# Group-norm moments of x in the prologue: half of the groups moved from VectorE to ScalarE and TensorE

## The chip, the cores and the metric

The kernel runs on one core of one Trainium2 chip. The metric is the device time of one execution in microseconds (us); the time given for a kernel is the median of its runs.

## The reference

Two attention layers, each behind a group norm with a residual add, on x of shape (1, 128, 256, 256) in fp32. Cut to what matters:

```python
def _gn(v, G=32, eps=1e-5):                    # 32 groups of 8 channels
    g = v.reshape(B_, H_, W_, G, C_ // G)
    m = jnp.mean(g, axis=(1, 2, 4), keepdims=True)   # over all rows and the 8 channels
    s = jnp.var(g, axis=(1, 2, 4), keepdims=True)
    return ((g - m) / jnp.sqrt(s + eps)).reshape(v.shape)

x = x + _L0_conv_ref(_gn(x), z, ...)   # row attention, 8 heads; bias b = layer_norm(z) @ Wb.T
x = x + _L1_conv_ref(_gn(x), ...)      # banded attention, 4 heads, |i - j| <= 16
return x
```

Layer 0 needs the mean and variance of every group of x over the whole tensor before its first row can be normalised. It also needs the bias b, made from z of shape (1, 256, 256, 128), before its first softmax.

## The kernel before

The kernel has a prologue, then layer 0, then layer 1. Layers 0 and 1 walk over 64 pairs of rows. The change lies in the prologue alone, except for its effect on when layer 0 can start.

**The loop of the prologue.** It runs over 16 z jobs (`zjobs`, n = 0 to 15) of 2 MB each. In the turn of job n:

- `z_front(n)` loads the z tile `zt` (three buffers, SyncE's queue, L1090), takes its row moments on VectorE (`bn_stats`, L1107), and has GpSimd raise the variances to the power -1/2 (`zrs`, L1115);
- `z_back(n-1)` transposes the z tile of the job before on TensorE (L1128, 32 transposes into the three PSUM tiles `ps_t`), copies the transposes to SBUF on ScalarE (`zT`, L1130, 8 copies), and multiplies them by the small weight (`z_project`, L1143). The projection runs half a job behind. Every second job also makes a copy `bT` (L1152), a scaling `bt` on VectorE (L1161) and eight exponentials into `eb` on ScalarE (`z_exp`, L1172);
- `x_block(n-1)`, in the turns n = 1 to 8, loads 4 MB of x into `xa` (two buffers, SyncE's queue, L1179) and takes the moments of its 32 groups on VectorE: 16 `bn_stats`, each of two groups (L1181).

`weights()` prepares the weights in steps between these. `load(4)` issues four small weight loads on ScalarE's queue (L832) in each of the turns 1 to 5, before that turn's `z_back`.

**After the eighth block of x** (n = 8, held in `ended`), a hand-written `plan` attaches steps to places (turns after `ended`, quarter of that turn's `z_front`; quarter 4 is the end of the turn). `begin` runs `x_moments`, which merges the blocks' moments on VectorE; `moments_steps` then averages over partitions on TensorE (`gps_l`, L972 and L981), and `norm` makes M0 and R0. `weigh` takes the moments of layer 0's first pair and calls `root` on GpSimd (`lrs`, L1288) and `send`, one quarter later in the plan, sends the result to DRAM from ScalarE's queue (L1294).

From n = 8 on, `z_back(n)` is also done in its own turn. Before the change this happens after `x_block`:

```python
            if nx < n and nx < nga:
                x_block(nx)
                ...
            if ended is not None:
                z_back(*behind)
                behind = None
            mark(4)
```

The prologue runs in a written order: each engine executes its instructions in the order of this text. An engine that waits holds up everything that follows on it. The prologue ends where layer 0 makes its first scores (`ps_sc`, L1367).

The functions that the diff touches, and what calls them:

Of the kernel before, what the change touches and what calls it, by code (L numbers as in the profile page):

```python
# [9 lines left out]
F32 = mybir.dt.float32  # L10
AF = mybir.ActivationFunctionType
ALU = mybir.AluOpType
AX = mybir.AxisListType
# [3 lines left out]
P = 128  # L17
# [4 lines left out]
def bcast(ap, axis, n):  # L22

    ap = ap.unsqueeze(axis)
    shape = list(ap.shape)
    shape[axis] = n
    return ap.broadcast_to(shape)
# [746 lines left out]
def fast_kernel(  # L774
# [25 lines left out]
    nc = tc.nc  # L800
    S, I, C = x.shape
# [4 lines left out]
    G = 32  # L806
    GE = C // G
    NB = I // P
# [12 lines left out]
    ones = const.tile([P, P], F32, name="ones")  # L821
    nc.vector.memset(ones, 1.0)
    avg = const.tile([P, P], F32, name="avg")
# [6 lines left out]
    def load(n):  # L830
        for _ in range(min(n, len(queued))):
            nc.scalar.dma_start(*queued.pop(0))  # L832
# [80 lines left out]
    GA = min(16, S)  # L913
# [17 lines left out]
    for a in range(KC):  # L931
        for h in range(H1):
            n = P // H1
# [5 lines left out]
    for h in range(H1):  # L939
        n = P // H1  # L940
# [22 lines left out]
    def group_pairs(src, g):  # L963

        return src[:, :, g * GE : (g + 2) * GE].rearrange("p n (h e) -> p n e h", h=2)

    def moments_steps(run, n, pool, psum, tag):

        ps = psum.tile([P, 512], F32, name=f"gps_{tag}", tag="mm")
        mean_p = pool.tile([P, G], F32, name=f"mean_{tag}", tag="gn_a", bufs=1)  # L970
        nc.vector.tensor_copy(mean_p, run[:, :, 1])
        nc.tensor.matmul(ps[:, :G], avg, mean_p, start=True, stop=True)  # L972
        yield
        mu = pool.tile([P, G], F32, name=f"mu_{tag}", tag="gn_b", bufs=1)
        nc.vector.tensor_copy(mu, ps[:, :G])
        d = pool.tile([P, G], F32, name=f"d_{tag}", tag="gn_c", bufs=1)
        nc.vector.tensor_sub(d, mean_p, mu)
        nc.vector.tensor_mul(d, d, d)
        nc.vector.scalar_tensor_tensor(d, run[:, :, 2], 1.0 / n, d, ALU.mult, ALU.add)
        ps2 = psum.tile([P, 512], F32, name=f"gps2_{tag}", tag="mm")  # L980
        nc.tensor.matmul(ps2[:, :G], avg, d, start=True, stop=True)  # L981
        yield
        rs = pool.tile([P, G], F32, name=f"rs_{tag}", tag="gn_d", bufs=1)
        nc.vector.tensor_scalar_add(rs, ps2[:, :G], 1e-5)
        nc.gpsimd.tensor_tensor(rs, rs, mhalf[:, :G], ALU.pow)
        yield
        M = const.tile([P, C], F32, name=f"M_{tag}")
        R = const.tile([P, C], F32, name=f"R_{tag}")
        for dst, src in ((M, mu), (R, rs)):
            nc.vector.tensor_copy(dst.rearrange("p (g e) -> p g e", e=GE), bcast(src, 2, GE))  # L990
        yield M, R

    pz = tc.alloc_tile_pool(name="pre_z", bufs=1, side="right")
    px = tc.alloc_tile_pool(name="pre_x", bufs=1, side="left")
    ps_mm = tc.alloc_tile_pool(name="ps_mm", bufs=2, space=PSUM)
    pps = tc.alloc_tile_pool(name="pre_ps", bufs=2, space=PSUM)

    def mm(name):
        return ps_mm.tile([P, 512], F32, name=name, tag="mm")
# [71 lines left out]
        nc.vector.tensor_add(bout_r, bout_r, ps[:, :C])  # L1071

    nga = S // GA
    st0 = pz.tile([P, nga, G, 3], F32, name="st0")

# [40 lines left out]
    def z_back(b, i0, zt, rs):  # L1118

        nonlocal turned  # L1120
        at = i0 % IS
        for j in range(at // 16, (at + IB) // 16):
            zTs = []
            for g in range(4):
                ps_t = pps.tile([P, 512], F32, name="ps_t", tag="zT", bufs=3)
                i = (4 * j + g) * 4 - at
                for a in range(4):
                    nc.tensor.transpose(ps_t[:, a * P : (a + 1) * P], zt[:, i + a, :], ident)  # L1128
                zT = pz.tile([P, 512], F32, name="zT", tag="zT", bufs=10)
                nc.scalar.copy(zT, ps_t)  # L1130
                zTs.append(zT)
            z_project()
            turned = (b, i0 - at, rs, j, zTs)

    def z_project():
        nonlocal turned, ps_b
        if turned is None:
            return
        (b, i0, rs, j, zTs), turned = turned, None
        if j == 0:  # L1140
            ps_b = pps.tile([P, 512], F32, name="ps_b", tag="bias", bufs=1)
        for g in range(4):
            nc.tensor.matmul(  # L1143
                ps_b[32 * g : 32 * (g + 1), :], wbz[:, j].rearrange("p a h -> p (a h)"), zTs[g],
                start=(j == 0), stop=(j == 3),
            )
        if j == 1:
            z_exp()
        if j < 3:
            return  # L1150
        bT = pz.tile([P, 512], F32, name="bT", tag="bT", bufs=2)
        nc.scalar.copy(bT, ps_b)  # L1152
        ps_k = pps.tile([P, 4, 4, 4, H], F32, name="ps_k", tag="keys", bufs=1)
        for a in range(4):
            nc.tensor.transpose(
                ps_k[:, a].rearrange("p g j h -> p (g j h)"), bT[:, a * P : (a + 1) * P], ident
            )
        bt = pz.tile([P, IS, H], F32, name="bt", tag="bt", bufs=2)
        for j in range(4):
            q = slice(j * 16, (j + 1) * 16)  # L1160
            nc.vector.tensor_tensor(  # L1161
                bt[:, q, :].rearrange("p (g a) h -> p g a h", g=4), ps_k[:, :, :, j, :].rearrange("p a g h -> p g a h"),
                bcast(rs[:, q].rearrange("p (g a) -> p g a", g=4), 3, H), ALU.mult,
            )
        weighed.append((b, i0, bt))
# [11 lines left out]
    def x_block(j):  # L1177
        xa = px.tile([P, GA * NB, C], F32, name="xa", tag="xa", bufs=2)
        nc.sync.dma_start(xa, x[j * GA : (j + 1) * GA].rearrange("s i c -> (s i) c").rearrange("(p n) c -> p n c", p=P))  # L1179
        for g in range(0, G, 2):  # L1180
            nc.vector.bn_stats(st0[:, j, g : g + 2, :].rearrange("p g f -> p (g f)"), group_pairs(xa, g))  # L1181

    def x_moments():

        each = GA * NB * GE
        run = pz.tile([P, G, 3], F32, name="run0")
        d = pz.tile([P, nga, G], F32, name="run0_d")
        nc.vector.tensor_reduce(run[:, :, 1], st0[:, :, :, 1].rearrange("p j g -> p g j"), AX.X, ALU.add)
        nc.vector.tensor_scalar_mul(run[:, :, 1], run[:, :, 1], 1.0 / nga)
        nc.vector.tensor_tensor(d, st0[:, :, :, 1], bcast(run[:, :, 1], 1, nga), ALU.subtract)  # L1190
        nc.vector.scalar_tensor_tensor(d, d, float(each), d, ALU.mult, ALU.mult)
        nc.vector.tensor_tensor(d, d, st0[:, :, :, 2], ALU.add)
        nc.vector.tensor_reduce(run[:, :, 2], d.rearrange("p j g -> p g j"), AX.X, ALU.add)
        return moments_steps(run, nga * each, pz, ps_mm, "l0")

# [355 lines left out]
    def weigh():  # L1553
# [5 lines left out]

    plan = {  # L1560
        (0, 4): begin, (1, 1): lambda: next(steps), (1, 3): lambda: next(steps), (1, 4): take, (2, 3): norm,
        (3, 4): weigh,
        (4, 2): lambda: now.send(nc.scalar),
        (4, 4): lambda: now.turn([mm("ps_x") for _ in range(KC)]),
        (5, 2): lambda: now.fetch(nc.scalar),
# [4 lines left out]
    ended = None  # L1570

    def mark(quarter):
        if n == 1 and quarter < 4 or n == 6:
            next(prepare, None)
        if ended is not None:
            plan.pop((n - ended, quarter), nothing)()


    behind, nx, n = None, 0, 0
    prepare = weights()  # L1580
    with tc.manual_schedule():
        zts = [z_load(*zjobs[0], 2)]
        load(8)
        zts.append(z_load(*zjobs[1]))
        for n, job in enumerate(zjobs):
            front = z_front(*job, zts.pop(0) if zts else z_load(*job))
            if n == 0:
                next(prepare)
                next(prepare)
            else:  # L1590
                load(4)
                if n == 1:
                    next(prepare)
            if behind is not None:
                z_back(*behind)
            behind = (*job, *front)
            if nx < n and nx < nga:
                x_block(nx)
                nx += 1
                if nx == nga:  # L1600
                    ended = n
            if ended is not None:
                z_back(*behind)
                behind = None
            mark(4)
        assert not plan
        z_project()
        z_exp()
        for f in ("centre", "scale"):
            getattr(nxt, f)()  # L1610
        for r in range(2):
            nxt.moments(r)
# [115 lines left out]
    with tc.tile_pool(name="l1", bufs=2) as sb, tc.tile_pool(  # L1728
        name="l1s", bufs=4
    ) as sm, tc.tile_pool(name="ps1_s", bufs=4, space=PSUM) as ps_s, tc.tile_pool(  # L1730
        name="ps1_o", bufs=1, space=PSUM
    ) as ps_o:

        def mm1(name):
            return ps_s.tile([P, 512], F32, name=name, tag="s")
# [348 lines left out]
        ps = mm1("ok_ps")  # L2084
# [67 lines left out]
```

## Time and profile before

| what | value |
|---|---|
| time before, median of 3 runs | 3188.46 us (3186.13 to 3190.39) |
| the profiled execution, its own time | 3190.91 us |
| its span in the trace | 3189.1 us |
| TensorE, VectorE, GpSimd, ScalarE busy over the span | 95%, 73%, 71%, 49% |
| first `ps_sc` matmul (end of the prologue) | 237.83 us from the span's start |
| VectorE on x's moments (`st<-xa`) | 128 instructions, 77.2 us |
| VectorE on z's moments (`zst<-zt`) | 256 instructions, 87.4 us |
| ScalarE's copies `zT` | 128 instructions, 66.9 us |

A row of the groups view reads: line, engine, operation, names, output shape, input shape, count, then busy us and mean ns of one, then the engine's idle time just ahead of these and what ended it. A row of the timeline reads: start in us, length in us, engine, line, operation, names, shapes, count, and in brackets the idle time before it with what ended that. Rows of the timeline merge several instructions.

### The profile page before, as it was taken

What the parts mean: (1) busy time and instruction counts of PE and PEld (TensorE: products, weight loads), DVE (VectorE), ACT (ScalarE), POOL (GpSimd) and SP (SyncE); (2) the same over time, 40 slices, a digit from 0 to 9 for tenths busy, and PEclk for the clock granted to TensorE, in tenths of its full rate; (3) what the DMA queues carried; (4) which work ended last, traced back from release to release, by engine and by line L of the source; (5) the groups of instructions that cost most, each with busy time, mean ns of one, the idle gap of its engine ahead of it and who ended that gap; (6) DMA issues with size and microseconds to landing.
All of it is one profiled execution on the core that took longest, in us unless ns stands there. A gap on an engine that the chain in (4) does not pass through costs nothing. (4 is left out here: it accounts for less than half of the span.)

```text
span 3189.1 us, 82775 instructions
## 1 busy us (share of the span) xinstructions
PE 3041.5 (95%) x34924; PEld 2086.6 (65%) x34924; DVE 2332.1 (73%) x3783; ACT 1551.1 (49%) x2501; POOL 2277.3 (71%) x1634
## 2 busy tenths in 40 slices
PE   4479999999999999999999999799999999999998
PEld 3245555555555555555555555588888888888886
DVE  7965677777777777777777777577777766666677
ACT  2354444444444444444444444355555555555553
POOL 3378888888988898888898987455555555555553
PEclk9789999999999999999999999899999999999999
DMA  9942333333333332333333432543434344434341
GB/s 349 393 159 53 70 91 96 97 71 95 96 97 71 98 93 66 93 91 97 71 97 94 97 71 61 108 101 82 102 82 96 87 95 88 96 88 93 90 96 47
DMA packets 691068, 328.56 MB, mean 103 GB/s; under 512 B 538656, under 2 KB 639904, under 8 KB 689536
## 3 DMA queue, kind: packets, MB, share of 16 engines
q1 hardware_dynamic: 686112, 320.28, 39.4%
q8 instruction: 276, 4.52, 0.6%
q10 hardware_dynamic: 4576, 2.90, 0.3%
q14 instruction: 104, 0.85, 0.1%
HBM read 254.36 MB, written 68.75 MB: 101 GB/s over the span
## 5 line engine op out<-in xcount | busy, mean ns | idle before, releaser
L1391 POOL TENSOR_TENSOR eboth<-e 128x512 f32<-128x512 f32 x512 | 743.4, 1472 | 186.6 <-PE ps_su L1410 100.4
L1387 DVE TENSOR_TENSOR e<-ps_sc,eb 128x1024 f32<-128x1024 f32 x384 | 458.3, 1221 | 297.4 <-ACT ps_sc L1379 297.4
L1908 POOL TENSOR_TENSOR e<-e,bw 128x384 f32<-128x384 f32 x256 | 258.0, 1028 | 501.1 <-ACT e L1906 501.1
L1379 ACT ACTIVATE ps_sc<-ps_sc 128x1024 f32<-128x1024 f32 x384 | 375.4, 1007 | 438.1 <-PE ps_sc L1367 314.0
L1367 PE MATMUL ps_sc<-qT,kT 32*128 32x256 f32 x4096 | 293.4, 400 | 1.8 <-ACT kT L1337 1.8
L1457 PEld LDWEIGHTS ps_y<-wo,oT 128*128 128x128 f32 x1024 | 195.3, 191 | 88.1 <-issue 44.4
L1333 PE MATMUL ps_p<-xnT,wq 128*128 128x512 f32 x512 | 249.4, 610 | 3.5 <-POOL xnT L1320 3.4
L1367 PEld LDWEIGHTS ps_sc<-qT,kT 32*128 32x128 f32 x4096 | 185.1, 184 | 103.2 <-issue 91.9
L1457 PE MATMUL ps_y<-wo,oT 128*128 128x256 f32 x1024 | 243.9, 381 | 7.1 <-POOL oT L1447 6.3
L1966 PE MATMUL ps_su_y<-w_out,oT 128*128 128x256 f32 x1024 | 244.7, 382 | 4.7 <-DVE odd L1944 2.8
L1333 PE MATMUL ps_p<-xgT,wg 128*128 128x512 f32 x512 | 248.9, 609 | 0.0
L1402 PE MATMUL ps_ov<-e,v 128*32 128x256 f32 x4096 | 248.7, 383 | 0.0
L1852 ACT ACTIVATE u<-ps_qk,bin_c 128x256 f32<-128x256 f32 x378 | 177.8, 478 | 132.3 <-PE ps_qk L1847 124.3
L1348 PE MATMUL ps_v<-wv,xnT 128*128 128x256 f32 x1024 | 241.9, 379 | 0.0
L1333 PE MATMUL ps_p<-xnT,wk 128*128 128x512 f32 x512 | 241.5, 594 | 0.0
L1883 PE MATMUL ps_v<-w_in,xgT 128*128 128x256 f32 x1024 | 238.3, 386 | 0.0
L1348 PEld LDWEIGHTS ps_v<-wv,xnT 128*128 128x128 f32 x1024 | 194.7, 190 | 55.1 <-issue 32.1
L1945 DVE RECIPROCAL rv<-odd 128x256 f32<-128x256 f32 x128 | 224.4, 1753 | 4.4
L1966 PEld LDWEIGHTS ps_su_y<-w_out,oT 128*128 128x128 f32 x1024 | 195.7, 191 | 32.9 <-DVE odd L1944 3.5
L1883 PEld LDWEIGHTS ps_v<-w_in,xgT 128*128 128x128 f32 x1024 | 189.3, 190 | 32.8 <-issue 0.5
L1402 PEld LDWEIGHTS ps_ov<-e,v 128*32 128x32 f32 x4096 | 120.4, 110 | 109.5 <-issue 43.9
L1847 PE MATMUL ps_qk<-dT,wst 128*128 128x256 f32 x756 | 187.7, 388 | 0.0
(201 smaller groups left out, 6027.7 us busy)
## 6 DMA issues: line engine op xcount, KB each, us to landing
xa<-in_x_dram SPq DMA_DIRECT2D x8, 4096.0 KB
xt<-in_x_dram SPq DMA_DIRECT2D x64, 512.0 KB
x<-xo SPq DMA_DIRECT2D x16, 2048.0 KB
xs<-x SPq DMA_DIRECT2D x256, 128.0 KB
xt<-x SPq DMA_DIRECT2D x64, 512.0 KB
rvb<-rsum SPq DMA_DIRECT2D x252, 128.0 KB
out_dram<-yo SPq DMA_DIRECT2D x63, 512.0 KB
xs<-in_x_dram SPq DMA_DIRECT2D x248, 128.0 KB
```

Source lines behind the costliest of these rows:

```text
L1333: nc.tensor.matmul(ps, w[:, k, m * P : (m + 1) * P], getattr(self, src)[:, k, :], start=(k == 0), stop=(k == KC - 1),)
L1348: nc.tensor.matmul(self.ps_v[:, b * C : (b + 1) * C], self.xnT[:, k, t * P : (t + 1) * P], wv[:, k, :], start=(k == 0), stop=(k == KC - 1),)
L1367: nc.tensor.matmul(self.pss[q // 2][:, q % 2, b, :], self.kT[rs, c, r * I + b * P : r * I + (b + 1) * P], self.qT[rs, c, r * I : (r + 1) * I],
L1379: nc.scalar.activation(self.pss[a], ps, AF.Exp)
L1387: nc.vector.tensor_tensor(es[a], pss[a], eb[:, h : h + 2], ALU.mult)
L1391: nc.gpsimd.tensor_tensor(t, es[a][:, :, 0, :], es[a][:, :, 1, :], ALU.add)
L1402: nc.tensor.matmul(ov[q * D0 : (q + 1) * D0, c, :], self.v[:, r, b, h * D0 : (h + 1) * D0], es[q // 2][:, q % 2, b, :], start=(b == 0), st ...
L1457: nc.tensor.matmul(self.ps_y[:, b * C : (b + 1) * C], self.oT[r][:, k, b * P : (b + 1) * P], wo[:, k, :], start=(k == 0), stop=(k == KC - 1),)
L1883: nc.tensor.matmul(ps[:, b * C : (b + 1) * C], self.xgT[:, k, t * P : (t + 1) * P], w_in[:, k, 2 * C : 3 * C], start=(k == 0), stop=(k == ...
L1908: nc.gpsimd.tensor_tensor(e[:, q], e[:, q], bcast(bw.rearrange("p b w -> p (b w)"), 1, KC), ALU.mult)
L1945: nc.vector.reciprocal(self.rv[:, r, :], odd[:, 2, :])
L1966: nc.tensor.matmul(ps[:, b], self.oT[r][:, k, b * P : (b + 1) * P], w_out[:, k, :], start=(k == 0), stop=(k == KC - 1),)
```

## The change

1. `x_block` gives VectorE only the first 16 groups: 8 `bn_stats` in place of 16.
2. For the other 16 groups ScalarE runs one `Square` activation per group over 256 elements of each partition, with a bias column `nm0` (minus a first guess of the mean) and an accumulated output `sq0`. The squares themselves go to a tile `junk` of one buffer. TensorE sums the same channels over all partitions with a matrix of ones (8 matmuls of 512 columns in four groups of 32 output partitions, accumulated in `ps_sx` over all blocks).
3. In the first block, `nm0` is made: one matmul by `avg` over four rows, one reduction and one scaling on VectorE.
4. `x_moments` and `moments_steps` merge both kinds. A second moment about the guess becomes a variance by subtracting the square of (mean minus guess).
5. In turn 8, `z_back(8)` is issued ahead of `x_block(7)` and not after it.
6. `weigh` moves in the plan from (3, 4) to (3, 3), a quarter of a turn earlier.

```diff
     def x_block(j):
         xa = px.tile([P, GA * NB, C], F32, name="xa", tag="xa", bufs=2)
         nc.sync.dma_start(xa, ...)
-        for g in range(0, G, 2):
+        for g in range(0, HG, 2):
             nc.vector.bn_stats(st0[:, j, g : g + 2, :].rearrange("p g f -> p (g f)"), group_pairs(xa, g))
+        if j == 0:
+            ps = mm("ps_m0")
+            nc.tensor.matmul(ps, avg, xa[:, 0:4, HX], start=True, stop=True)
+            nc.vector.tensor_reduce(nm0, ps.rearrange("p (n g e) -> p g n e", n=4, e=GE), AX.XY, ALU.add)
+            nc.vector.tensor_scalar_mul(nm0, nm0, -1.0 / (4 * GE))
+        each = GA * NB // 4
+        for i in range(each):
+            q = i % 4
+            nc.tensor.matmul(
+                ps_sx[32 * q : 32 * (q + 1), :], ones[:, :32], xa[:, 4 * i : 4 * (i + 1), HX],
+                start=(j == 0 and i < 4), stop=(j == nga - 1 and i >= each - 4),
+            )
+        for g in range(HG):
+            at = (HG + g) * GE
+            junk = pz.tile([P, GA * NB, GE], F32, name="junk", tag="junk", bufs=1)
+            nc.scalar.activation(
+                junk, xa[:, :, at : at + GE], AF.Square, bias=nm0[:, g : g + 1], accum_out=sq0[:, j, g : g + 1]
+            )
```

```diff
     def moments_steps(mean_p, m2, n, pool, psum, tag):
...
-        nc.vector.tensor_sub(d, mean_p, mu)
+        nc.vector.tensor_sub(d[:, :HG], mean_p[:, :HG], mu[:, :HG])
+        nc.vector.tensor_add(d[:, HG:], mu[:, HG:], nm0)
         nc.vector.tensor_mul(d, d, d)
-        nc.vector.scalar_tensor_tensor(d, run[:, :, 2], 1.0 / n, d, ALU.mult, ALU.add)
+        nc.vector.scalar_tensor_tensor(d[:, :HG], m2[:, :HG], 1.0 / n, d[:, :HG], ALU.mult, ALU.add)
+        nc.vector.scalar_tensor_tensor(d[:, HG:], m2[:, HG:], 1.0 / n, d[:, HG:], ALU.mult, ALU.subtract)
...
     def x_moments():
...
+        nc.vector.tensor_reduce(
+            mean_p[:, HG:], ps_sx.rearrange("p (n g e) -> p g n e", n=4, e=GE), AX.XY, ALU.add
+        )
+        nc.vector.tensor_scalar_mul(mean_p[:, HG:], mean_p[:, HG:], 1.0 / (32 * nga * each))
+        nc.vector.tensor_reduce(m2[:, HG:], sq0.rearrange("p j g -> p g j"), AX.X, ALU.add)
```

```diff
-        (3, 4): weigh,
+        (3, 3): weigh,
...
             behind = (*job, *front)
+            if ended is not None or nx == nga - 1 and nx < n:
+                z_back(*behind)
+                behind = None
             if nx < n and nx < nga:
                 x_block(nx)
...
-            if ended is not None:
-                z_back(*behind)
-                behind = None
             mark(4)
```

More of the change, by code (lines that the diff above doesn't have):

```diff
@@ L965, in group_pairs, with moments_steps @@
         return src[:, :, g * GE : (g + 2) * GE].rearrange("p n (h e) -> p n e h", h=2)
-    def moments_steps(run, n, pool, psum, tag):
+    def moments_steps(mean_p, m2, n, pool, psum, tag):
         ps = psum.tile([P, 512], F32, name=f"gps_{tag}", tag="mm")
-        mean_p = pool.tile([P, G], F32, name=f"mean_{tag}", tag="gn_a", bufs=1)
-        nc.vector.tensor_copy(mean_p, run[:, :, 1])
         nc.tensor.matmul(ps[:, :G], avg, mean_p, start=True, stop=True)
@@ L1073, in fast_kernel @@
     nga = S // GA
-    st0 = pz.tile([P, nga, G, 3], F32, name="st0")
+    HG = G // 2
+    HX = slice(HG * GE, C)
+    st0 = pz.tile([P, nga, HG, 3], F32, name="st0")
+    sq0 = pz.tile([P, nga, HG], F32, name="sq0")
+    nm0 = pz.tile([P, HG], F32, name="nm0")
+    ps_sx = pps.tile([P, 512], F32, name="ps_sx", tag="sx", bufs=1)
     IB, IS = 32, 64
@@ L1183, in x_moments @@
     def x_moments():
         each = GA * NB * GE
[L1186 to L1190, printed above, removed]
+        mean_p = pz.tile([P, G], F32, name="run0")
+        m2 = pz.tile([P, G], F32, name="run0_m2")
@@ L1191, in x_moments @@
+        d = pz.tile([P, nga, HG], F32, name="run0_d")
+        mean_d = mean_p[:, :HG]
+        nc.vector.tensor_reduce(mean_d, st0[:, :, :, 1].rearrange("p j g -> p g j"), AX.X, ALU.add)
+        nc.vector.tensor_scalar_mul(mean_d, mean_d, 1.0 / nga)
+        nc.vector.tensor_tensor(d, st0[:, :, :, 1], bcast(mean_d, 1, nga), ALU.subtract)
         nc.vector.scalar_tensor_tensor(d, d, float(each), d, ALU.mult, ALU.mult)
         nc.vector.tensor_tensor(d, d, st0[:, :, :, 2], ALU.add)
-        nc.vector.tensor_reduce(run[:, :, 2], d.rearrange("p j g -> p g j"), AX.X, ALU.add)
@@ L1194, in x_moments @@
-        return moments_steps(run, nga * each, pz, ps_mm, "l0")
+        nc.vector.tensor_reduce(m2[:, :HG], d.rearrange("p j g -> p g j"), AX.X, ALU.add)
+        nc.vector.tensor_reduce(
[3 more added lines that the diff above has]
+        nc.vector.tensor_reduce(m2[:, HG:], sq0.rearrange("p j g -> p g j"), AX.X, ALU.add)
+        return moments_steps(mean_p, m2, nga * each, pz, ps_mm, "l0")
```

## The prediction

> **What bounds the kernel now.** I read the timeline of the first 240 us first, since every edit lies there, then the windows of 10 us, the waits of SyncE's queue, and the groups for durations. From 237.83 us on, layer 0 runs with TensorE busy nine tenths and more of the time, so a shift of that moment passes through to the end one for one. The question is what sets 237.83.
>
> ```profile
> 87.56 9.60 DVE L1181 BATCH_NORM_STATS2 st<-xa 128x6 f32<-128x512 f32 x16 [1.02 <-DMA xa<-in_x_dram]
> 97.08 5.35 DVE L1107 BATCH_NORM_STATS2 zst<-zt 128x6 f32<-128x256 f32 x16
> 103.38 9.61 DVE L1181 BATCH_NORM_STATS2 st<-xa 128x6 f32<-128x512 f32 x16
> ...
> 151.87 9.60 DVE L1181 BATCH_NORM_STATS2 st<-xa 128x6 f32<-128x512 f32 x16
> 161.39 0.87 DVE L1161 TENSOR_TENSOR bt<-ps_k,zrs 128x128 f32<-128x128 f32 x4
> ```
>
> VectorE in the timeline: a turn is 9.6 us on x and 5.4 us on z, some 16 us in all, without a hole from 87.6 to 161. That looks like a VectorE bound. But the trace also holds the updates of the DMAs' semaphores: the blocks xa0 to xa7 land at 33.66, 50.70, 71.33, 87.53, 103.35, 119.15, 134.91 and 150.78. The last four steps are 15.8 us each, and the z tiles land between them (109.36, 125.03, 140.91), each transfer beginning where the one before ends: 9.9 us for 4 MB of x, 5.9 for 2 MB of z. VectorE starts 0.03 to 1.9 us after each landing. **DMA and VectorE are level**; a faster VectorE alone gains about 1 us plus half of the last block.
>
> ```profile
> 90.00:100.00 10.00, 0.00 (x0) 0.00 (x0) 10.00 (x22) 0.00 (x0) 2.04 (x1) 0.60 1.09 451
> 150.00:160.00 10.00, 0.15 (x4) 0.00 (x0) 9.97 (x21) 0.12 (x1) 5.43 (x1) 0.67 1.09 355
> ```
>
> Windows (PE, PEld, DVE, ACT, POOL busy, clock, DMA share, GB/s): VectorE and DMA are full, TensorE and ScalarE empty. So there is room for the moved work on average.
>
> ```profile
> 167.37 0.63 PE L981 MATMUL gps_l<-d_l,avg 128*128 128x32 f32 x2 [1.47 <-DVE d_l L979]
> 167.81 3.25 PE L1128 MATMUL ps_t<-ident,zt 128*128 128x128 f32 x16
> ...
> 169.00 0.58 ACT L1130 COPY zT<-ps_t 128x512 f32<-128x512 f32 x1 [18.88 <-PE ps_t L1128]
> ...
> 199.70 1.56 ACT L1130 COPY zT<-ps_t 128x512 f32<-128x512 f32 x3 [8.36 <-DMA rs_d<-rsT]
> ```
>
> From the second averaging matmul (167.37) on, the bound is the pair TensorE/ScalarE: seven `z_back` (9 to 15) with almost no hole until 237.83, since they could not start before that matmul. The one large hole is 8.36 us before 199.70: ScalarE waits to issue `send`. Behind it:
>
> ```profile
> 186.01 10.84 POOL L1115 TENSOR_TENSOR zrs<-zrs,mhalf 128x32 f32<-128x32 f32 x2
> 196.80 1.03 POOL L1288 TENSOR_TENSOR lrs<-lrs,mhalf 128x4 f32<-128x4 f32 x1
> 197.86 0.21 DVE L1292 STREAM_TRANSPOSE rsT<-lrs 128x32 f32<-128x32 f32 x1 [5.32 <-POOL lrs L1288]
> ```
>
> The root of 1.03 us stands behind two powers of 5.42 us on GpSimd.
>
> **What the Trainium skill says.** *ScalarE: Activation LUTs*, section "What ACT_TABLE_LOAD costs": an ACTIVATE with a pointer bias takes about 280 ns + 0.833 ns per element, and two in a row overlap by about 93 ns. The trace agrees: `u<-ps_qk` (128x256) has a mean of 478 ns against 493, and eight exponentials of mean 404 ns took 2.46 us, a step of 294 ns. *VectorE: DVE Perf Modes*, section "Two Vector instructions with no wait between them", says that an accumulator output makes two instructions, the second a read; whether ScalarE pays likewise no page tells, and no row shows it. *TensorE: Matmul & The Clock Gate*, "What's actually happening": an idle TensorE drops to half clock. The trace agrees: after the hole up to 60.0, 16 transposes took 3.65 us, and 2.0 us when warm. *DMA: Bandwidth & Descriptors*, "Queues, rings and completion order": the SyncE and ScalarE queues share the 16 engines in turn. The trace agrees: `bv_c`, tiny, issued on ScalarE at 53.60, landed at 70.19 among the large loads.
>
> **The change part by part.**
>
> VectorE loses 64 of the 128 `bn_stats`, 64 x 0.60 us (9.60 / 16) = 38.6 us. Hidden: DMA still lands a block every 15.8 us.
>
> TensorE gains 64 matmuls of 512 columns in four column groups. The nearest row is `ps_b`, eight such in 1.06 us when warm; it counts two instructions a matmul, so 8 matmuls are 2.1 us a block, 17 us in all, beside the squares. They wait for the block's landing, and the transposes of the next `z_back` queue behind them, but ScalarE is busy with squares then. Cost nothing while squares take over 4 us.
>
> **ScalarE gains 128 squares**, in order with the `zT` copies. The step s of one: 0.40 us (493 - 93 ns) plus the accumulator read. Bounds: nothing, or the whole fixed 280 ns with no overlap; I take 0.15, so **s = 0.55 (0.40 to 0.68)**, 8.8 us a block. ScalarE per turn: 8.8 + `z_back`, which is 6.2 us with `bT` (126.11 to 132.34) and 6.7 with exponentials (118.44 to 125.18): 15.3 on average, also level with DMA's 15.8. So three engines are level, and the sum has to be made along ScalarE:
>
> - first square at 41.3: half of the first block's statistics (35.36 + 4.9), the guess's reduction (estimate 0.85, from 0.58 for 256 elements) and scaling (0.17); the matmul for it runs beside;
> - 128 squares: 70.4;
> - `z_back` 1 to 8, all of which now stand ahead of the last squares: 5.0 + 3 x 6.7 + 4 x 6.2 = 49.9;
> - ScalarE's own issues of the small loads (`w_out` to `bout_r`), which now stand between squares: 6.3.
>
> The last square ends at 167.9. Every block has landed by then, and each has slack: xa5's buffer is free at about 131, and xa7, which takes it, gets its turn on the DMA engines only at 140.91. After the squares: a reduction (0.3, estimate), four z statistics (1.41), six small operations (1.4): the second averaging matmul at 171.0 against 167.37: **+3.7**. The merging arithmetic of the other half is done before, while VectorE waits.
>
> TensorE idles some 5 us in each turn while ScalarE squares. `z_back(4)`, started cold, took 7.6 us (78.99 to 86.56) and not 6.2. Two of eight that way: **+2.8** (bounds 0 and 11).
>
> `z_back(8)` ahead of `x_block(7)`: it fills a wait for xa7 if ScalarE waits, and otherwise delays the squares; its time is in the sum. `bt`, on VectorE ahead of the last statistics, waits for it; hidden, VectorE has 9 us.
>
> `weigh` a quarter earlier: `xg` is ready at 186.08, VectorE comes there at 186.5. The root then runs after one power (191.4 to 192.5), VectorE reaches `rsT` at 192.6, `send` is issued by 194.4: ScalarE goes on at 194.5 and not at 199.70: **-5.2**. The z power moved behind the root ends 1 us later; its reader `bt` (205.25) does not notice. The DMA in `weigh` (xt) keeps its place between the same z loads on SyncE. What is late next is the chain of copies, without a hole that size.
>
> Sum: 3.7 + 2.8 - 5.2 = **+1.3 us**. It is made against the profiled execution of 3190.91 us (span 3189.1), 2.45 above the median, so I carry the difference to the median: 3188.46 + 1.3 = 3189.8 us.
>
> **Rivals.** The comparison can tell about 0.2%, 6.4 us, from no change.
>
> Slower, by the accumulator read. Each 0.01 us in s costs 128 x 0.01 = 1.3 us, since the chain holds all 128. If the read waits for the pipeline, s is 0.60 to 0.68: +8 to +18, up to 3206. It decides from s = 0.59. For it: in VectorE's merge (162.17 to 165.03) an operation that reads the result of the one before starts only after its end. Against it: the step of the exponentials, which overlap. Chance 0.25.
>
> Slower, by the small loads. DMAs take turns on eight semaphores, and each waits for the one before on its own:
>
> ```profile
> SPq L1179 <- DMA bv_c<-in_b_in_dram: 16.9, 1, 16.9
> ```
>
> SyncE held xa3 for `bv_c`, issued by ScalarE, and xa2 for a `w_out` in the same way. If the same pairs share semaphores after the change, these small loads come only after the squares of blocks 1 and 2 (65.6 and 88.9): DMA runs dry, xa3 lands near 107 and not at 87.53, the last square ends near 185, and the sum is about +15, 3204. Against it: ScalarE's loads fall behind SyncE's in time, so that the pairs are likely dealt anew. A table load per switch to Square (1.28 us in the trace's one row, a dozen of them) would cost as much. Together 0.10.
>
> Faster: s is 0.48 or less. ScalarE waits for DMA: xa6 at 134.9, squares 6.4 to 7.7, two `z_back` 12.9, squares: the end at 161 to 163, the matmul 1 to 4 us early, with `weigh` -6 to -9: 3180 to 3182. A dry spell of DMA from 48.5 to 52, where zt3 waited for a shared semaphore, may vanish and give some more. Chance 0.20.
>
> No change within 0.2%: s from 0.49 to 0.59. Chance 0.45.
>
> **The numbers.** Likeliest 3189.8. Range 3179 (DMA's floor) to 3206 (unoverlapped read, which also covers most of the small loads' case). Faster 0.20, same 0.45, slower 0.35.
>
> **What would show it.** Right: `st<-xa` with 64 instructions, about 38 us; squares in steps of 0.55 us; ScalarE nearly full from 41 to 168; the second averaging matmul at about 171 to 174; ScalarE's wait before `send` about 3 us; first `ps_sc` at about 239. Wrong: holes in ScalarE ahead of the squares that end with a landing of `xa` (DMA bound), SyncE waiting for a small load, squares stepping by over 0.6 us, or table loads.

## The result, and the profile after

| | before | after |
|---|---|---|
| median | 3188.99 us (6 runs, 3186.13 to 3190.39) | 3203.39 us (6 runs, 3199.36 to 3208.75) |
| the profiled execution, its own time | 3190.91 us | 3208.75 us |
| second averaging matmul (`gps_l`, L981 in both) | 167.37 | 190.93 |
| first `ps_sc` | 237.83 | 255.68 |
| from the one to the other | 70.46 | 64.75 |

The change makes the kernel slower: ratio 1.0049, 95% interval 1.0037 to 1.006, about 14 us. The profiled execution of after is the slowest of its six, 5.4 us above their median, and that of before lies 1.9 us above its own, so distances between the traces (17.85 us at the first `ps_sc`, 17.84 in the profiled times) overstate the typical loss by some 3 us.

The timeline of after, where the prologue ends (start, length, engine, line, and in brackets the idle time before with what ended it):

```profile
190.93 0.63 PE L981 MATMUL gps_l<-d_l,avg 128*128 128x32 f32 x2 [6.05 <-DVE d_l L979]
...
209.57 5.44 POOL L1120 TENSOR_TENSOR zrs<-zrs,mhalf 128x32 f32<-128x32 f32 x1
...
214.96 1.02 POOL L1318 TENSOR_TENSOR lrs<-lrs,mhalf 128x4 f32<-128x4 f32 x1
...
218.03 2.05 ACT L1135 COPY zT<-ps_t 128x512 f32<-128x512 f32 x4 [2.88 <-DMA rs_d<-rsT]
...
255.68 1.15 PE L1397 MATMUL ps_sc<-qT,kT 32*128 32x256 f32 x16
```

The root (`lrs`) now stands behind one power and not two, and ScalarE's hole at `send` is 2.88 us instead of 8.36. All of the loss lies ahead of 190.93. The windows at the same places as before (PE, PEld, DVE, ACT, POOL busy, clock, DMA share, GB/s):

```profile
90.00:100.00 10.00, 9.16 (x54) 4.96 (x55) 6.45 (x19) 8.94 (x24) 5.11 (x2) 0.67 1.01 379
150.00:160.00 10.00, 8.52 (x55) 5.58 (x53) 9.27 (x23) 7.45 (x21) 0.00 (x0) 0.77 0.95 375
```

ScalarE, empty before, is busy for 8.94 of the 10 us of the first window (TensorE's 9.16 are at a granted clock of 0.67). From 40 to 188 us it is the fullest engine: 119.6 of 148 us, against 83.5 on TensorE and 80.5 on VectorE. The groups by shape of after, ScalarE, first 250 us (busy us, mean ns of one, idle before):

```profile
L1202 ACT ACTIVATE junk<-xa,nm 128x256 f32<-128x256 f32 x128 | 65.1, 508 | 7.3 <-DVE nm L1191 3.4
L1202 ACT ACTIVATION_READ_ACCUMULATOR junk<-xa,nm 128x1 f32 x128 | 24.0, 187 | 0.0
```

A square with an accumulated output is two instructions. Their order in the timeline of after:

```profile
82.55 0.51 ACT L1202 ACTIVATE junk<-xa,nm 128x256 f32<-128x256 f32 x1
82.97 0.19 ACT L1202 ACTIVATION_READ_ACCUMULATOR junk<-xa,nm 128x1 f32 x1
83.18 0.51 ACT L1202 ACTIVATE junk<-xa,nm 128x256 f32<-128x256 f32 x1
83.60 0.19 ACT L1202 ACTIVATION_READ_ACCUMULATOR junk<-xa,nm 128x1 f32 x1
```

From square to square is 0.634 us, not the 0.55 of the prediction. A block of 16 takes 10.1 us, and ScalarE never waits for a block of x. It is the other way round, as SyncE's waits in the first 200 us of after show (us in total, times, longest):

```profile
SPq L1184 <- ACT junk L1202: 41.4, 6, 10.3
```

The longest waits of SyncE for x are these. Each load of `xa` waits until the squares two blocks earlier have freed its buffer (they are issued at 50.56, 68.21, 88.87, 107.74, 127.92 and 145.30, each within 0.05 us of the end of a block of squares). So in this stretch the loads of x follow ScalarE, and no longer the other way.

One part of the traces differs where the code does not, and the readings below have to allow for it. In the stretch from the second averaging matmul to the first `ps_sc`, TensorE waits for the same things and as long in after and in the kernel with two buffers of `junk` (below). In the first trace its granted clock then falls (0.57 from 222 to 227 us), in the second it does not (1.00 from 202.6 to 207):

```profile
218.67 0.66 PE L1133 MATMUL ps_t<-ident,zt 128*128 128x128 f32 x4 [1.81 <-ACT zT L1135]
222.59 3.62 PE L1133 MATMUL ps_t<-ident,zt 128*128 128x128 f32 x16
```

```profile
199.32 0.66 PE L1133 MATMUL ps_t<-ident,zt 128*128 128x128 f32 x4 [1.81 <-ACT zT L1135]
202.17 1.99 PE L1133 MATMUL ps_t<-ident,zt 128*128 128x128 f32 x16
```

The stretch takes 64.75 us in after and 61.96 in the other. All traces with the moved `weigh` have one of these two lengths, 64.8 to 65.0 (after, `weigh` alone, no squares, TensorE sums the squares) or 61.8 to 62.0 (the others). A difference of up to 3 us between two traces can be this alone.

### The profile page after: what moved, and what is told of

Read it like the earlier page. It is cut to its first block, busy times and chain, and to the rows that moved or that the text cites. A ratio compares the mean times of both kernels' runs of the same rounds, so it can differ in the third digit from the quotient of the medians.

```text
span 3207.0 us, 83179 instructions
## 1 busy us (share of the span) xinstructions
PE 3067.6 (96%) x35054; PEld 2098.9 (65%) x35054; DVE 2295.7 (72%) x3725; ACT 1627.9 (51%) x2757; POOL 2277.8 (71%) x1634
```

## The experiments

Theory: ScalarE's chain in program order (squares, copies of `z_back`, issues) sets the end. Rivals: the late blocks of x, the sums on TensorE or its clock, the new place of `z_back(8)`. Ratios are to the kernel before, measured on the same chip beside each. Differences from after in us go across chips, on which the kernel before took 3188.73 to 3190.5.

**weigh alone** (the kernel before with its place in the plan changed).

```diff
-        (3, 4): weigh,
+        (3, 3): weigh,
```

> The kernel before with one edit: weigh at (3, 3) instead of (3, 4); all moments stay on VectorE. My theory: the part of the change that gains is weigh, since ScalarE's 8.36 us wait ahead of send becomes about 3 us: 5 to 6 us faster than before, about 3183, with the first ps_sc at 232 to 233. Rival: the chain of zT copies is held by something else next and the gain is under 2 us.

Measured 3181.36 us, ratio 0.9979 (0.997 to 0.9987). From the second averaging matmul to the first `ps_sc` it takes 65.0 us instead of 70.46. So the move of `weigh` gains by itself.

**The change without the move of weigh.**

> The kernel after with weigh put back to (3, 4): the move of the moments alone. My theory: the move of weigh gains in both kernels about the same, so this is 5 to 7 us slower than after: 3208 to 3211, some 20 us slower than before. Rival (the gain of weigh in the kernel before came from a state of the queues that the change has altered): same as after, 3203.

Measured 3208.25 us, ratio 1.0059 (1.0045 to 1.0072), 4.9 us above after by the medians and 3 us by the ratios, whose intervals overlap. ScalarE's hole at `send` is back with 8.10 us, and the stretch from the second averaging matmul to the first `ps_sc` takes 70.16 us instead of 64.75. So the move of the moments costs about 19 us, and the move of `weigh` returns 3 to 5 of them.

**No squares** (the loop of squares taken out, `sq0` set once).

> The kernel after without the squares (the second moments of ScalarE's half are left out, sq0 is a constant set once); the sums by ones on TensorE and everything else stay. My theory: nothing but ScalarE's chain makes the change slow, so that DMA bounds here: the second averaging matmul at about 160, 8 us faster than before with weigh moved alone (3181.36), so about 3173. Rival (the sums on TensorE or the new order of z_back(8) cost by themselves): no faster than weigh moved alone.

Measured 3176.20 us, ratio 0.9958 (0.9945 to 0.9972), with the second averaging matmul at 161.4. With `weigh` alone it stands at 166.54, so that the change without its squares brings 5 us there. The sums by ones, the guess and the new order of `z_back(8)` cost nothing that shows; the loss is in the squares. This is also about the least that cheaper squares can reach.

**No accumulator** (the sums of squares are left out, `sq0` set once).

```diff
-                junk, xa[:, :, at : at + GE], AF.Square, bias=nm0[:, g : g + 1], accum_out=sq0[:, j, g : g + 1]
+                junk, xa[:, :, at : at + GE], AF.Square, bias=nm0[:, g : g + 1]
```

> The kernel after, with the 128 squares kept but without accum_out (the sums of squares are left out; sq0 is a constant set once). My theory: the bound after the change is ScalarE's chain, and the accumulator read is what makes a square 0.634 us instead of about 0.40. Without it a block of squares takes 6.5 us, ScalarE needs some 14 us a turn, DMA bounds again, and the second averaging matmul comes at 163 to 167 instead of 190.93: 24 to 28 us faster than after, 3176 to 3180. Rival (cold TensorE or late x blocks make the loss, and the read overlaps): at most 8 us faster than after, not faster than before.

Measured 3189.05 us, ratio 1.0001 (0.9992 to 1.0009): 14 us below after, half of what I expected. The timeline shows why:

```profile
58.56 8.61 ACT L1203 ACTIVATE junk<-xa,nm 128x256 f32<-128x256 f32 x16
```

A block takes 8.61 us, a step of 0.541 us, without any read. So the read was not the whole excess over 0.40. In the trace's records each square waits for a semaphore that ScalarE itself raises with the square before (or with its read, where there is one), since all write the one buffer of `junk`. The times agree: a square of 0.508 us is followed by the next 0.541 us after its start, thus 0.03 us after its end, and in after the next one also starts 0.03 us after the end of the read.

**Two buffers of junk**

```diff
-            junk = pz.tile([P, GA * NB, GE], F32, name="junk", tag="junk", bufs=1)
+            junk = pz.tile([P, GA * NB, GE], F32, name="junk", tag="junk", bufs=2)
```

> The kernel after with one number changed: the tile junk, which takes the squares that nobody reads, gets two buffers instead of one. In the kernel after each square waits on ScalarE's own semaphore for the one before, as both write the same buffer; here it waits for the one before that. My theory: this wait keeps two squares from overlapping and makes most of the step of 0.634 us; the step falls to about 0.50 to 0.54, the chain loses 12 to 17 us, and the kernel is 10 to 15 us faster than after, 3188 to 3193. Rival: the accumulator read itself drains the pipeline, the wait adds nothing to it, and the step and the time stay (3203).

Measured 3188.31 us, ratio 1.0001 (0.9992 to 1.0009): 15 us below after by one number. (The profiled execution, 3182.28 us, is the fastest of its thirteen, so its trace shows a larger gain than the medians.) The timeline:

```profile
59.04 0.20 ACT L1202 ACTIVATION_READ_ACCUMULATOR junk<-xa,nm 128x1 f32 x1
59.13 0.51 ACT L1202 ACTIVATE junk<-xa,nm 128x256 f32<-128x256 f32 x1
59.53 0.20 ACT L1202 ACTIVATION_READ_ACCUMULATOR junk<-xa,nm 128x1 f32 x1
59.62 0.51 ACT L1202 ACTIVATE junk<-xa,nm 128x256 f32<-128x256 f32 x1
```

A square starts 0.09 us after the start of the read before it, so inside it; in after it starts 0.21 us after. The step is 0.491 us. The median includes the gain of `weigh`: against `weigh` alone (3181.36 us) the move of half of the groups still costs 7 us.

**Both**: two buffers, no accumulator.

> The kernel after with two buffers of junk and without accum_out (the sums of squares are left out; sq0 is a constant set once): the fourth corner beside one buffer with the accumulator (step 0.634 us), one buffer without it (0.541) and two buffers with it (0.491). My theory: the wait on the one buffer costs about 0.14 and the accumulator read about 0.09, and the two add up: the step is 0.40, the figure from which the prediction started, a block takes 6.5 us, ScalarE needs less than DMA's 15.8 us a turn, and the kernel comes to 3176 to 3182. Rival (squares do not overlap as the exponentials do): the step stays at 0.49 and the time at 3188.

Measured 3175.31 us, ratio 0.9956 (0.9942 to 0.9969), level with the kernel without squares. The group of its squares (busy us, mean ns of one):

```profile
L1203 ACT ACTIVATE junk<-xa,nm 128x256 f32<-128x256 f32 x128 | 51.9, 505 | 3.5 <-DVE nm L1192 3.5
```

The four corners of the step:

| step of a square, us | one buffer of `junk` | two buffers |
|---|---|---|
| with the accumulator | 0.634 | 0.491 |
| without | 0.541 | 0.399 |

The two costs add up: the wait on the single buffer costs 0.14 us a square, the accumulator read 0.09. The rival of this run (squares don't overlap as the exponentials do) falls: with two buffers and no accumulator the next square starts 0.106 us before the end of the one before.

**TensorE kept warm** (20 matmuls by zeros ahead of the fourth group of transposes of `z_back`).

```diff
+                if g == 3 and j == at // 16 and 0 < nx < nga:
+                    for k in range(20):
+                        q = k % 4
+                        nc.tensor.matmul(
+                            ps_sx[32 * q : 32 * (q + 1), :], nought, zt[:, i : i + 4, :], start=False, stop=False
+                        )
```

> The kernel after, with 20 matmuls by zeros of 512 columns, accumulated into ps_sx, put ahead of the fourth group of transposes of z_back(1) to z_back(8), so that TensorE is busy while ScalarE squares. My theory: the gaps between the blocks of squares (66.9 us for z_back and issues, of which about 8 are due to transposes at half clock) shrink by 5 to 8 us, and the kernel is 5 to 8 us faster than after, about 3196. Rival (the chain from transpose to copy is not slowed by the clock, or the matmuls by zeros are in the way): no change, or some us slower.

Measured 3205.68 us, ratio 1.0046 (1.0032 to 1.006): no difference from after. It did not test the question in most places: TensorE idled another 3.4 to 4.0 us and was cold again, and the matmuls in `z_back(8)` lay on the path. So again with 36, and none in `z_back(8)`:

> As the kernel with 20 matmuls by zeros, but with 36 of them and none in z_back(8), where no squares stand ahead of it. In the first try TensorE still sat idle for 3.4 to 4.0 us before most groups of transposes and was cold again, and the matmuls in z_back(8) lay on the path. My theory: now the gaps between blocks of squares shrink by 0.7 to 2 us each, 5 to 9 us in seven, and the kernel is 5 to 9 us faster than after, 3194 to 3198. Rival (half clock does not set these gaps): no change from after, 3203.

Measured 3201.62 us, ratio 1.0041 (1.0027 to 1.0054), not to be told from after in time. The traces say more. The same step of `z_back` in after and then with 36 matmuls:

```profile
90.84 1.11 PE L1133 MATMUL ps_t<-ident,zt 128*128 128x128 f32 x4 [7.77 <-ACT zT L1135]
91.89 1.94 PE L1148 MATMUL ps_b<-zT,wbz 128*32 128x512 f32 x8
93.75 3.35 PE L1133 MATMUL ps_t<-ident,zt 128*128 128x128 f32 x16
```

```profile
89.81 0.66 PE L1141 MATMUL ps_t<-ident,zt 128*128 128x128 f32 x4 [0.76 <-ACT zT L1143]
90.39 1.06 PE L1156 MATMUL ps_b<-zT,wbz 128*32 128x512 f32 x8
91.39 1.53 PE L1141 MATMUL ps_t<-ident,zt 128*128 128x128 f32 x12
```

The same matmuls take a little over half the time, and the granted clock from 69 to 98 us is 1.00 instead of 0.64. Four gaps of ScalarE between blocks of squares (those ahead of the third, fourth, fifth and seventh block) fall from 10.57, 8.78, 10.07 and 9.25 us to 7.23, 7.54, 6.76 and 6.58: 10.6 us for four `z_back`. Not all of that need be the clock: in the kernel with `weigh` put back, whose squares are the same and which has no filler, these four are 10.23, 7.97, 8.09 and 8.87, only 7.0 us above the filler's. And the gap ahead of the sixth block grew from 7.29 to 14.26, since there the filler itself came late:

```profile
118.18 2.07 PE L1069 MATMUL ps_bo<-w_out,bv_w 128*128 128x256 f32 x4 [3.79 <-DVE bv_w L1066]
120.04 2.77 PE L1141 MATMUL ps_t<-ident,zt 128*128 128x128 f32 x12
122.74 8.63 PE L1137 MATMUL ps_sx<-zt,nought 128*32 128x512 f32 x72
131.30 0.66 PE L1141 MATMUL ps_t<-ident,zt 128*128 128x128 f32 x4
```

TensorE had waited for `bv_w`, so 8.63 us of zeros stood ahead of the transposes that ScalarE needed. So the cold clock costs about 1.8 to 2.6 us in each of those four gaps. All seven gaps together are 67.0 us in after, 64.8 with the filler and 64.4 with `weigh` put back; that a net gain in time can be had from warming TensorE is not shown.

**The old place of z_back(8).**

> The kernel after with z_back(8) issued after x_block(7), as in the kernel before. In the kernel after no landing of xa is waited for, so z_back(8), ahead of the last squares, delays them by its 6 to 7 us. My theory: the last squares end 6 to 7 us earlier, but z_back(8) then follows them ahead of the other seven, so ScalarE's sum up to the first ps_sc stays: within 3 us of after. Rival (the second averaging matmul alone sets the end): 6 us faster than after, 3197.

Measured 3203.37 us, ratio 1.0047 (1.0033 to 1.006): as after. The last square ends at 179.08 instead of 188.24, but the second averaging matmul comes at 190.30, no earlier, for a reason that I had not seen. VectorE in that trace:

```profile
184.08 0.88 DVE L1166 TENSOR_TENSOR bt<-ps_k,zrs 128x128 f32<-128x128 f32 x4 [19.39 <-PE ps_k L1160]
184.88 0.37 DVE L1213 TENSOR_REDUCE run<-st 128x16 f32<-128x128 f32 x1
```

`bt` of `z_back(8)` stands ahead of `x_moments` in VectorE's order and waits 19.39 us for a product that now comes after the squares. The rival was therefore not tested: the matmul did not come earlier.

**TensorE sums the squares too** (4 squares of 1024 elements a block, without bias and accumulator, 16 matmuls by ones).

```diff
+        for h in range(4):
+            sq = pz.tile([P, part, C - HG * GE], F32, name="sq", tag="sq", bufs=1)
+            nc.scalar.activation(sq, xa[:, h * part : (h + 1) * part, HX], AF.Square)
+            for i in range(part // 4):
+                ... # ones x xa into two column groups of ps_sx, ones x sq into the other two
```

> The kernel after, with ScalarE squaring a quarter of a block (8 rows of 16 groups, 1024 elements) in one instruction, without bias and accumulator, and TensorE adding up the squares by ones as well as x (16 matmuls a block instead of 8). 4 squares a block at about 1.05 us are 4.2 us of ScalarE in place of 10.15. My theory: DMA bounds again, the second averaging matmul comes at 163 to 167: 24 to 28 us faster than after, about 3177, and 10 us faster than before. Rival: the 8 more matmuls a block, at half clock, hold up the transposes of z_back by 4 us a block and eat most of the gain: no faster than before.

Measured 3194.74 us, ratio 1.0017 (1.001 to 1.0023): 9 us better than after, not the 26 expected. Its timeline:

```profile
75.78 1.06 ACT L1191 ACTIVATE sq<-xa 128x1024 f32<-128x1024 f32 x1 [1.23 <-PE ps_sx L1196]
78.06 1.06 ACT L1191 ACTIVATE sq<-xa 128x1024 f32<-128x1024 f32 x1 [1.23 <-PE ps_sx L1196]
```

I repeated the fault under study: `sq` has one buffer, so each square but the first of a block waits 1.23 us (twice 2.10) until TensorE has read the one before, and a block takes 8 to 9 us. After the last of them the copies of `z_back` wait about 3 us more in most turns, as the transposes stand behind the sums.

**A quarter of the groups** (8 on ScalarE and TensorE, 24 on VectorE).

```diff
-    HG = G // 2
+    HG = G - 8
...
```

The rest of the edit fits the shapes to 8 groups: a matmul by ones takes 8 rows instead of 4, so that a block needs 4 of them instead of 8, and the guess is made from 8 rows.

> The kernel after, with ScalarE and TensorE given 8 groups instead of 16 (HG = G - 8; 4 matmuls and 8 squares a block), VectorE 24 (12 bn_stats). My theory: 8 squares at 0.634 us are 5.1 us, with some 8 us of z_back and issues 13.1 us a turn, below DMA's 15.8: DMA bounds, the second averaging matmul comes at 163 to 166, 3178 to 3181, about level with weigh moved alone and 8 to 10 us faster than before. Rival (the interleaving of squares with z_back on ScalarE costs in itself, however few squares there are): no faster than before.

Measured 3175.64 us, ratio 0.9961 (0.9947 to 0.9974): faster than both kernels. The windows 80 to 140 us, of after and then of this one:

```profile
80.00:140.00 60.00, 36.58 (x228) 21.30 (x220) 39.55 (x106) 50.38 (x148) 19.00 (x4) 0.74 0.90 324
```

```profile
80.00:140.00 60.00, 38.44 (x248) 22.03 (x247) 52.30 (x126) 43.97 (x122) 21.71 (x4) 0.84 1.05 395
```

ScalarE falls from 50.4 to 44.0 of 60 us, VectorE rises to 52.3, and DMA's share from 0.90 to 1.05: the DMA engines are full again, as in the kernel before (1.04). The second averaging matmul stands at 161.82. With `weigh` alone the kernel before has 3181.36; the intervals of the two just overlap (0.9947 to 0.9974 and 0.997 to 0.9987). Each of the five runs here (3174.0 to 3177.56) lies below each of the twelve there (3179.71 to 3185.98), though on another chip (the kernel before took 3189.25 and 3188.73 us on the two), so that sharing the moments very likely gains some 5 us on top of `weigh`.

**A quarter and two buffers.**

> 8 groups on ScalarE and TensorE, as in the kernel with HG = G - 8, and two buffers of junk besides. My theory: with 8 squares a block ScalarE no longer bounds, so a step of 0.49 in place of 0.634 gains nothing: within 2 us of that kernel's 3175.64. Rival (ScalarE still bounds there): 8 us faster, since 64 squares lose 0.14 us each.

Measured 3174.95 us, ratio 0.9954 (0.9941 to 0.9968): the same. The step falls from 0.64 to 0.49 us here too, and nothing is gained: the wait on the single buffer, worth 15 us where ScalarE bounds, is worth nothing where it has room.

## Why the prediction was right and where it failed

The time lies in the range, and the sign of the likeliest case was right, but its size was not: no change within 0.2% had 0.45, and the outcome, +0.49%, was the ground of the slower rival with 0.25. That it is in the range is in part luck: the upper end was set for squares that do not overlap because of the read, and what filled it was another wait and longer gaps. Its own steps, against the trace of after:

| step | predicted | trace | difference |
|---|---|---|---|
| first square | 41.3 | 40.43 | -0.9 |
| 128 squares | 70.4 | 80.8 | +10.4 |
| `z_back` 1 to 8, issues, cold clock (49.9 + 6.3 + 2.8) | 59.0 | 67.0 | +8.0 |
| last square to the second averaging matmul | 3.1 | 2.7 | -0.4 |
| from there to the first `ps_sc` (`weigh`) | -5.2 | -5.7 | -0.5 |
| sum | +1.3 | +17.9 | +16.6 |

**The step that failed is s = 0.40 + 0.15.** The 0.40 was right for squares that overlap (0.399 with two buffers and no accumulator), and the read cost 0.09, less than the 0.15 allowed. What was left out is the wait of each square for the one before, 0.14 us. The text named the page of the Trainium skill, *ScalarE: Activation LUTs*, "What ACT_TABLE_LOAD costs", for two activations in a row that overlap by about 93 ns, and supported it with eight exponentials. The measurement agrees where the buffers alternate (0.505 us long in a step of 0.399: 106 ns), but the exponentials write eight different slices of `eb`, while the squares write one buffer. The front of this document even says that `junk` has one buffer; I priced the instruction and not its write.

**The slower rival was right in number and wrong in reason.** It set 0.60 to 0.68 by a read that waits for the pipeline. The step was 0.634, but by a wait for a buffer, mostly; with two buffers the next square starts inside the read. Its price of 1.3 us for each 0.01 us of the step would have put the sum at +12 us; the trace has 17.9, and the rest lies mostly in the gaps.

**The cold clock was mis-sized.** The prediction put two cold `z_back` of eight, +2.8, with 11 as the upper bound. TensorE idles after its third group of transposes until ScalarE has squared, in seven turns (52.1 us in all), and its next four transposes take 1.11 to 1.12 us each time, against 0.66 after a wait of 0.74 us. In five of these gaps the following 16 transposes are slow as well; the filler shows 7 to 10.6 us in four gaps. *TensorE: Matmul & The Clock Gate*, "What's actually happening", says that an idle TensorE drops to half its clock; this trace agrees (3.34 to 3.62 us for 16 transposes in those five gaps against 1.99). What was wrong was the count of places. How much of the 8.0 us it makes stays open, since the gaps differ from trace to trace (67.0 us here, 64.4 with `weigh` put back).

**What held.** VectorE's shorter part gained nothing while ScalarE bounded. Without the squares the second averaging matmul comes 5.1 us earlier than with `weigh` alone (161.4 against 166.54), near the 1 us and half of a block that the prediction gave for a faster VectorE. TensorE's sums took 1.9 us a block (2.1 predicted) and were hidden, as the kernel without squares confirms. In the traces `weigh` gave 5.4 us inside the change and 5.5 outside (5.2 predicted; 4.9 and 7.4 by the medians). The small loads did not decide: SyncE still waited for some (27.5 us for `w_out` and `bo_r`), but mostly ahead of loads of z, as the semaphores were dealt anew, and no square waited for a landing of x. ScalarE loads a table once in the prologue, in both kernels. DMA did not land "a block every 15.8 us", since the loads of x waited for the squares; that follows from the first fault. The link from step to time held as well: "no change" was set for 0.49 to 0.59, and the kernels with 0.491 and 0.541 are at ratio 1.0001.

## What to carry to other kernels

An output that nobody reads still has a buffer. Here many short instructions in a row wrote the same one, each waited for the one before, and the engine lost its overlap: give such a tile two buffers, or else do not take the price per instruction from a row whose outputs differ. When three engines are level, move only as much work as leaves the receiver below the resource that bounds anyway (here a quarter of the groups, not a half), and expect that work put into one engine makes another one wait for it, and TensorE slow after the wait.

## What the runs showed of the hardware

- An activation of ScalarE with an accumulated output is two instructions, the square (508 ns) and a read (187 ns); the read adds 0.09 us to the step, with either number of buffers.
- A wait of ScalarE for its own previous instruction costs 0.14 us: 0.634 against 0.491, and 0.541 against 0.399. With the wait the next square starts 0.03 us after the end of the one before; without it, 0.106 us ahead of that end.
- A handover from ScalarE to TensorE and back through one buffer of 1024 elements left ScalarE idle for 1.23 us ahead of most squares of 1.06 us.
- After the same waits of TensorE, the last of 1.81 us, 16 transposes took 3.62 us in one trace (granted clock 0.57) and 1.99 in another (1.00).
